# A transformer block with conditioning: the transfers of the weight sums issued by GpSimd at listed steps, and scores of the QKV stage placed mostly among V products

## The chip, the cores and the metric

The kernel runs on one core of a Trainium2 chip. The metric is device time in microseconds (us); lower is better. A core has five engines that run side by side, each with its own in-order queue of instructions: TensorE (PE in the profile; its weight loads are PEld), VectorE (DVE), ScalarE (ACT), GpSimd (POOL) and SyncE (SP). An engine waits at its next instruction until what that one needs is there, and all behind it wait too. That holds for an engine that issues a DMA as well: the transfer itself runs on 16 DMA engines, but its issue stands in the engine's queue. In this kernel SyncE issues nearly all DMAs.

## The reference

One block with adaptive layer norms: D = 512, 16 heads of 32, hidden width 2048, T = 2048 tokens in each of two batches. Cut to what matters:

```python
mod = silu(condition) @ Wada + bada
sh_a, sc_a, gt_a, sh_m, sc_m, gt_m = split(mod, 6)
xm = layernorm(x, g1, be1) * (1 + sc_a) + sh_a
x = x + gt_a * (softmax_causal(q @ k.T * scale) @ v @ Wproj + bproj)   # q, k, v = split(xm @ Wqkv)
xm = layernorm(x, g2, be2) * (1 + sc_m) + sh_m
x = x + gt_m * (gelu(xm @ W1 + b1) @ W2 + b2)
```

All is float32, and the attention is causal within a batch.

## The kernel before

The stages follow one another: QKV of batch 0, attention of batch 0, projection of batch 0, QKV of batch 1, its attention and projection, and then the two MLP layers for all tokens. The change touches the two QKV stages, and through them what is left to the attentions.

**QKV stage (class `Qkv`).** A batch has four groups g of 512 tokens, and a group has 12 steps n; in what follows a step is also counted through the stage, at = 12 g + n, from 0 to 47. Group 0 makes eight columns of Q and K by plain products and then four tiles of V (`values`, L868 on). Groups 1 to 3 make two tiles of V (steps 0 and 1), then two pairs of Q/K columns of four steps each (steps 2 to 5 and 6 to 9), each pair by two sets of seven block products in place of eight (`sevens`, L961 on, so 14 products a pair), and two more tiles of V (steps 10 and 11). The seven products need sums of weights (`weight_sums`, GpSimd, L928, in group 0) and sums of tokens (`token_sums`, GpSimd, L959, made for group g + 1 behind step 10 of group g). VectorE adds the partial products (`total`, L992) and makes the low half of each stored column (`keep`, L855 and L856), which SyncE stores (L861). Behind the first pair, or the first two columns in group 0, SyncE is told to load the keys and queries of this group back in the layout that the scores need (`asked`, `load_keys` L339, `load_queries` L348): the keys wait for the columns' store to land.

**Scores.** The attention needs the maximum of each row of scores ahead of its exponentials. So every score tile is computed once beforehand (`bank`: a product s<-kst,qst on PE into one of two PSUM buffers, and VectorE's maximum, L484, or with the causal mask L479), and a unit's maxima are split into three bf16 parts (`split`, L501 to L505). A unit is four heads and 512 queries; the units of the first four heads have 16, 32, 48 and 64 score tiles (units 0 to 3; unit u needs the keys of groups 0 to u and the queries of group u). The function `among`, called behind each product of the QKV stage, asks the planner (`count`, with a cost of width + 190 per tile, or + 250 with the mask) how many tiles bring the sum of costs up to a goal. Before, it begins at step 2 of each group: group 1 spreads unit 0 evenly over its ten steps, and groups 2 and 3 spread units 1 and 2 evenly over twenty; unit 2 may begin at step 7 of group 2. In attention the planner hands out the rest by due times (`due`): the cost still owed to each later unit over the weight of the steps left.

**Weight sums for the MLP.** The MLP multiplies by sums of quarters of W1 and W2, which are made beside the QKV stages. A quarter (class `Quarters`, 16 in all) is four loads (`load`, L1116, 128 KB each), four sums on GpSimd (`make`, L1128) and one store of 896 KB (`store`, L1136). Class `FirstLayer` then loads a block of W1's quarters (1 MB), makes four sums (L1158) and stores 1.75 MB (w1e, L1190), seven times in batch 1. The rooms in SBUF in which they lie are reused, so that a load waits for the landing of an earlier store. All these transfers are issued by SyncE, in the same queue as the columns' stores, the keys, the queries, the token rows x (L809) and Wada (L1289). The function `also(g, n)`, called at each step, says which of load, make and store runs there: before, by the step's remainder by 4 up to step 29 and by 2 from then on; 13 quarters are done in batch 0 and three, besides the seven W1 blocks, in batch 1. Tiles of batch 1's attention (its exponentials e, written by ScalarE at L619) lie where the two W1 rooms were.

Most instructions of a stage are kept in the order of the program; the loads of keys, queries and x and the columns' stores may be moved by the scheduler, which builds each engine's queue once.

Of the kernel before, what the change touches and what calls it, by code (L numbers as in the profile page):

```python
# [8 lines left out]
F32 = mybir.dt.float32  # L9
# [18 lines left out]
def dit_block_kernel(  # L28
# [768 lines left out]
    class Qkv:  # L797
# [241 lines left out]
        def run(self, hp, also):  # L1039
# [3 lines left out]
            for g in range(NG):  # L1043
# [26 lines left out]
                def among(n, k):  # L1070
                    if g > 0 and n >= 2:


                        past = 4 * (n - 2) + k + 1
                        if g == 1:
                            row.score(row.count(cum[0] * past / 40, 0))
                        else:
                            past += 40 * (g - 2)
                            row.score(
                                row.count(  # L1080
                                    cum[0] + (cum[2] - cum[0]) * past / 80,
                                    1 if g == 2 and n < 7 else 2,
                                )
                            )

# [9 lines left out]
    class Quarters:  # L1095
# [9 lines left out]
        def load(self, room):  # L1105
# [3 lines left out]
            for n, i, k in ((A11, 0, 0), (A12, 0, 1), (A21, 1, 0), (A22, 1, 1)):  # L1109
                if f < FC // 2:  # L1110
                    at = (f + i * FC // 2) * P
                    src = w1_v[:, k * C // 2 : (k + 1) * C // 2, at : at + P]
                else:
                    src = w2_v[:, f - FC // 2 + k * FC // 2, i * D // 2 : (i + 1) * D // 2]
                    src = src.rearrange("p (c d) -> p c d", d=P)
                act(nc.sync.dma_start(w[:, n], src))  # L1116
            self.loaded.append((f, w))
# [13 lines left out]
        def store(self):  # L1131
# [3 lines left out]
            act(  # L1135
                nc.sync.dma_start(  # L1136
                    dst.rearrange("p n c d -> p (n c) d"),
# [29 lines left out]
    class FirstLayer:  # L1167
# [8 lines left out]
        def load(self):  # L1176

            act(load_blocks(nc.sync, self.rooms[self.at % 2], 1, self.at))
            self.at += 1
# [8 lines left out]
        def store(self):  # L1188

            act(nc.sync.dma_start(w1e[self.stored], self.rooms[self.stored % 2]))  # L1190
            self.stored += 1
# [66 lines left out]
    with pool("wada") as wp, pool("qkv0") as qp, pool(  # L1258
# [108 lines left out]

        free, early = 2 * (C * 2 + MTT) + 5, 13

        def also(g, n):  # L1370

            at = g * (C * 2 + MTT) + n
            if 11 <= at <= free:
                if at % 4 == 3:
                    quarters.load(room[0])
                elif at % 4 == 0:
                    quarters.make()
                elif at % 4 == 1 and quarters.made:
                    quarters.store()
            if at >= free:  # L1380
                if at == free:
                    w = wp.tile([P, 2 * C * D], F32, tag="wada", name="w7")
                    room[:] = [w[:, k * piece : (k + 1) * piece] for k in range(2)]
                if at % 2 == 1 and quarters.at < early:
                    quarters.load(room[quarters.at % 2])
                elif at % 2 == 0:
                    if quarters.made:
                        quarters.store()
                    if quarters.loaded:
                        quarters.make()  # L1390
            if g == 0 and n == 2:
# [20 lines left out]
    with pool("qkv1") as qp, pool("ps_qkv1", bufs=6, space=PSUM) as ps_mm:  # L1412
# [20 lines left out]
        with pool("hl1") as hp:  # L1433
# [7 lines left out]
            def also(g, n):  # L1441
                at = g * (C * 2 + MTT) + n
                if at in (0, 1, 6):
                    quarters.load(part[(quarters.at - early) % 2])
                if at in (1, 2, 11):
                    quarters.make()
                if at in (3, 4, 13):
                    quarters.store()
# [6 lines left out]

            late_loads = (11, 15, 22, 26, 35, 39, 43)
            qkv.run(hp, also)
# [689 lines left out]
```

## Time and profile before

| | us |
|---|---|
| median of 3 runs | 2315.2 |
| lowest and highest of them | 2313.03, 2316.77 |
| profiled execution, its own time | 2319.8 |
| profiled execution, span from first to last instruction | 2318.1 |
| QKV stage of batch 0 (18.5 to 222.8 of the span) | 204.3 |
| attention of batch 0 (222.8 to 717.3) | 494.5 |
| QKV stage of batch 1 (805.1 to 995.3) | 190.2 |
| attention of batch 1 (995.3 to 1498.3) | 503.0 |
| rest behind it (1498.3 to 2318.1) | 819.8 |

How the rows are read. A row of the windows view has a stretch, its length, and for PE, PEld, DVE, ACT and POOL the busy us and the number of instructions, then the granted share of the TensorE clock, the DMA engines' busy share and GB/s. A row of the groups view has line, engine, operation, out<-in, shapes and count; then busy us and the mean in ns; then the engine's idle time just before these instructions, and what ended most of it. A row of the timeline has start, length, engine, line, operation and, in brackets, a longer idle time before it with what ended it. A row of the waits view has who waited for whom, the us in total, how many times and the longest. SPq and POOLq are queues that issue DMAs; a float32 matmul is recorded as two halves.

### The profile page before, as it was taken

Reading aid. Unit: us, or ns where it says so; the run is one execution under the profiler, and the core shown is the slowest. Engines: PE = TensorE matmul, PEld = TensorE weight load, DVE = VectorE, ACT = ScalarE, POOL = GpSimd, SP = SyncE. Lnnn points to the kernel's source line nnn. Section 1 sums busy time; section 2 is a strip of 40 time slices with the busy share of each in tenths; the row PEclk is TensorE's granted clock in tenths of the full one; section 3 lists DMA queues with packets and bytes.
Section 4 is the critical chain, followed back from the end, with each engine's and each line's share of the span. In section 5 each row is a group of like instructions: output and inputs, shape, how many; then the busy total and the mean of one; then the engine's idle time right before and its main releaser. Section 6 shows DMA issues by size and latency. Waiting matters only on the chain. (4 is left out here: it accounts for less than half of the span.)

```text
span 2318.1 us, 34368 instructions
## 1 busy us (share of the span) xinstructions
PE 2248.9 (97%) x12429; PEld 1443.0 (62%) x12429; DVE 1560.1 (67%) x3132; ACT 981.8 (42%) x1908; POOL 1279.0 (55%) x998
## 2 busy tenths in 40 slices
PE   8979999999999999999999999999999999999998
PEld 4656545555444456744455545446888888788887
DVE  3467776767765525766677677555896876877787
ACT  3323555555556134245555555632332242252230
POOL 3233787878884453258798787654764602602510
PEclk9999999999999999999999999999999999999999
DMA  7888605151143679781321513265375654554643
GB/s 255 250 229 255 131 24 119 47 118 43 35 141 108 237 224 315 243 228 33 79 68 34 123 29 126 90 216 199 121 273 205 208 176 156 199 174 152 216 144 116
DMA packets 153858, 355.66 MB, mean 153 GB/s; under 512 B 14496, under 2 KB 56012, under 8 KB 138968
## 3 DMA queue, kind: packets, MB, share of 16 engines
q1 hardware_dynamic: 151296, 336.90, 48.3%
q0 software_dynamic: 2016, 16.02, 1.7%
q8 instruction: 98, 1.61, 0.3%
q14 instruction: 72, 0.59, 0.1%
q10 hardware_dynamic: 376, 0.55, 0.1%
HBM read 253.80 MB, written 107.48 MB: 156 GB/s over the span
## 5 line engine op out<-in xcount | busy, mean ns | idle before, releaser
L619 ACT ACTIVATE e<-st 128x512 f32<-128x512 f32 (+1 forms) x1152 | 573.7, 578 | 404.5 <-PE st L204 357.3
L484 DVE TENSOR_REDUCE mx<-s 128x1 f32<-128x512 f32 x612 | 413.3, 687 | 225.3 <-PE s L204 223.8
L649 POOL TENSOR_TENSOR ee<-ee,e 128x1024 f32<-128x1024 f32 x212 | 499.0, 2388 | 7.7 <-ACT e L619 7.7
L204 PE MATMUL s<-kst,qst 128*128 128x512 f32 (+3 forms) x1032 | 438.1, 427 | 30.6 <-DMA qst<-q 11.5
L204 PE MATMUL st<-qst,kst 128*128 128x512 f32 (+3 forms) x1280 | 402.5, 379 | 0.0
L204 PE MATMUL ps_a<-sum,room 128*128 128x256 f32 x1504 | 358.3, 382 | 6.6 <-DVE c L1630 3.8
L204 PEld LDWEIGHTS ps_a<-sum,room 128*128 128x128 f32 x1504 | 282.3, 191 | 56.5 <-issue 8.7
L204 PE MATMUL o<-e,vv 128*32 128x512 f32 (+3 forms) x2560 | 301.8, 539 | 0.9 <-POOL e L628 0.9
L479 DVE CUSTOM_DVE_ANT_0 junk<-s,causal 128x128 bf16<-128x128 f32 (+3 forms) x420 | 205.9, 490 | 121.9 <-PE s L204 114.3
L204 PEld LDWEIGHTS s<-kst,qst 128*128 128x128 f32 x1032 | 195.1, 189 | 138.1 <-issue 45.5
L204 PEld LDWEIGHTS st<-qst,kst 128*128 128x128 f32 x1280 | 230.6, 189 | 68.6 <-issue 39.4
L649 POOL TENSOR_TENSOR ee<-e 128x1024 f32<-128x1024 f32 x84 | 198.2, 2383 | 119.3 <-ACT e L619 119.2
L204 PEld LDWEIGHTS <-sel 32*128 32x128 bf16 x1152 | 29.6, 91 | 196.0 <-issue 192.3
L628 POOL TENSOR_SCALAR_AFFINE_SELECT e<-e 128x256 f32<-128x256 f32 x256 | 104.4, 441 | 84.9 <-ACT e L619 51.9
L1858 POOL TENSOR_TENSOR c<-c,h 128x512 f32<-128x512 f32 x40 | 58.3, 1480 | 160.9 <-ACT c L1856 160.9
L204 PE MATMUL ps_b<-sum,room 128*128 128x256 f32 x608 | 143.6, 379 | 0.0
L204 PE MATMUL st<-fold,sel 32*128 32x512 bf16 (+1 forms) x1152 | 119.1, 373 | 8.6 <-ACT e L619 4.3
L204 PEld LDWEIGHTS ps_b<-sum,room 128*128 128x128 f32 x608 | 115.0, 190 | 15.4
L1128 POOL TENSOR_TENSOR w<-w 128x256 f32<-128x256 f32 x64 | 45.2, 729 | 142.0 <-DMA w<-in_L_cond_W_dram 130.2
L204 PEld LDWEIGHTS o<-e,vv 128*32 128x32 f32 x2560 | 61.4, 108 | 99.3 <-issue 80.3
L204 PE MATMUL ps_v<-wqkv,xmT 128*128 128x512 f32 x256 | 118.2, 597 | 0.0
L484 DVE TENSOR_REDUCE mx<-st 128x1 f32<-128x512 f32 x156 | 107.0, 686 | 3.8 <-PE st L204 1.3
(227 smaller groups left out, 3216.2 us busy)
## 6 DMA issues: line engine op xcount, KB each, us to landing
qst<-q SPq DMA_DIRECT2D x128, 256.0 KB
room<-w1e SPq DMA_DIRECT2D x28, 1024.0 KB
kst<-k SPq DMA_DIRECT2D x24, 1024.0 KB
room<-w1e SPq DMA_DIRECT2D x28, 768.0 KB
room<-w2e SPq DMA_DIRECT2D x21, 1024.0 KB
q<-hl SPq DMA_DIRECT2D x32, 512.0 KB
k<-hl SPq DMA_DIRECT2D x32, 512.0 KB
room<-w2e SPq DMA_DIRECT2D x21, 768.0 KB
```

Source lines behind the costliest of these rows:

```text
L204: return tc.keep_in_program_order(nc.tensor.matmul(*args, **kw))
L479: nc.vector.tensor_tensor_reduce(junk[:, :w], s[:, :w], causal[:, QB - w :], 1.0, MASKED, ALU.add, ALU.max, m,)
L484: nc.vector.tensor_reduce(m, s[:, :w], axis=AX.X, op=ALU.max)
L619: act(nc.scalar.activation(e[:, h % 2, :w], sts[h][:, :w], AF.Exp))
L628: nc.gpsimd.affine_select(d, d, pattern=[[0, 2], [1, P]], compare_op=ALU.is_ge, fill=0.0, base=0, channel_multiplier=-1,)
L649: act(engine.tensor_tensor(dst, x, y, ALU.add))
L1128: act(nc.gpsimd.tensor_tensor(w[:, n], w[:, x], w[:, y], op))
L1858: nc.gpsimd.tensor_tensor(c, c, piece_of(base, i, t, pair), ALU.add)
```

## The change

1. The loads and stores of `Quarters` and `FirstLayer` are issued by GpSimd instead of SyncE.
2. In batch 0 the steps of load, make and store are three lists, with 11 quarters instead of 13; the first is loaded at step 5 instead of 11. Within a step a store comes first, then a sum, then a load.
3. Batch 1 makes five quarters instead of three, and the W1 blocks are loaded at other steps; the last at 39 instead of 43, so its store stands at 43 instead of 47.
4. `among` begins at step 0 of groups 1 to 3. A V step counts three times a Q/K step: a group is 20 parts, of which the four V steps have 3 each and the eight Q/K steps 1 each. Group 1 still scores unit 0; groups 2 and 3 score unit 1 and, by cost, two thirds of unit 2; the rest goes to attention. Unit 2 may begin at step 8 of group 2.

```diff
                 def among(n, k):
-                    if g > 0 and n >= 2:
-                        past = 4 * (n - 2) + k + 1
-                        if g == 1:
-                            row.score(row.count(cum[0] * past / 40, 0))
-                        else:
-                            past += 40 * (g - 2)
-                            row.score(
-                                row.count(
-                                    cum[0] + (cum[2] - cum[0]) * past / 80,
-                                    1 if g == 2 and n < 7 else 2,
-                                )
-                            )
+                    if g == 0:
+                        return
+                    half = MTT // 2
+                    values = min(n, half) + max(0, n - half - 2 * C)
+                    past = 3 * values + min(max(0, n - half), 2 * C)
+                    among_values = n < half or n >= half + 2 * C
+                    past = (past + (3 if among_values else 1) * (k + 1) / 4) / 20
+                    if g == 1:
+                        row.score(row.count(cum[0] * past, 0))
+                        return
+                    goal = cum[1] + (cum[2] - cum[1]) * 2 // 3
+                    row.score(
+                        row.count(
+                            cum[0] + (goal - cum[0]) * (past + g - 2) / 2,
+                            1 if g == 2 and n < 8 else 2,
+                        )
+                    )
...
-                act(nc.sync.dma_start(w[:, n], src))
+                act(nc.gpsimd.dma_start(w[:, n], src))
...
-                nc.sync.dma_start(
+                nc.gpsimd.dma_start(
                     dst.rearrange("p n c d -> p (n c) d"),
...
-            act(load_blocks(nc.sync, self.rooms[self.at % 2], 1, self.at))
+            act(load_blocks(nc.gpsimd, self.rooms[self.at % 2], 1, self.at))
...
-            act(nc.sync.dma_start(w1e[self.stored], self.rooms[self.stored % 2]))
+            act(nc.gpsimd.dma_start(w1e[self.stored], self.rooms[self.stored % 2]))
...
-        free, early = 2 * (C * 2 + MTT) + 5, 13
+        free, early = 2 * (C * 2 + MTT) + 5, 11
+        loads = (5, 11, 15, 19, 23, 27, 29, 30, 35, 36, 40)
+        makes = (7, 12, 16, 20, 24, 28, 31, 32, 37, 38, 42)
+        stores = (9, 13, 17, 21, 25, 29, 33, 33, 39, 40, 44)
...
-            if 11 <= at <= free:
-                if at % 4 == 3:
-                    quarters.load(room[0])
-                elif at % 4 == 0:
-                    quarters.make()
-                elif at % 4 == 1 and quarters.made:
-                    quarters.store()
-            if at >= free:
-                if at == free:
-                    w = wp.tile([P, 2 * C * D], F32, tag="wada", name="w7")
-                    room[:] = [w[:, k * piece : (k + 1) * piece] for k in range(2)]
-                if at % 2 == 1 and quarters.at < early:
-                    quarters.load(room[quarters.at % 2])
-                elif at % 2 == 0:
-                    if quarters.made:
-                        quarters.store()
-                    if quarters.loaded:
-                        quarters.make()
+            if at == free:
+                w = wp.tile([P, 2 * C * D], F32, tag="wada", name="w7")
+                room[:] = [w[:, k * piece : (k + 1) * piece] for k in range(2)]
+            for step, steps in (
+                (quarters.store, stores), (quarters.make, makes),
+                (lambda: quarters.load(room[quarters.at % len(room)]), loads),
+            ):
+                for _ in range(steps.count(at)):
+                    step()
...
-                if at in (0, 1, 6):
+                if at in (0, 1, 6, 7, 14):
                     quarters.load(part[(quarters.at - early) % 2])
-                if at in (1, 2, 11):
+                if at in (1, 2, 11, 12, 16):
                     quarters.make()
-                if at in (3, 4, 13):
+                for _ in range((3, 4, 13, 13, 18).count(at)):
                     quarters.store()
...
-            late_loads = (11, 15, 22, 26, 35, 39, 43)
+            late_loads = (11, 20, 23, 27, 31, 35, 39)
```

A W1 block that is loaded at step a is summed at a + 2 and stored at a + 4, before and after.

## The prediction, on record before the run

> **What bounds the kernel now.** First the page's busy line, then the busy time of each engine by stage (QKV stage of batch 0, its attention, QKV stage of batch 1, its attention).
>
> ```profile
> span 2318.1 us, 34368 instructions
> PE 2248.9 (97%) x12429; PEld 1443.0 (62%) x12429; DVE 1560.1 (67%) x3132; ACT 981.8 (42%) x1908; POOL 1279.0 (55%) x998
> ```
>
> ```profile
> core 0: us, PE busy (x) PEld busy (x) DVE busy (x) ACT busy (x) POOL busy (x), PEclk, DMA share, GB/s
> 18.50:222.80 204.30, 188.36 (x713) 122.78 (x713) 102.49 (x262) 66.24 (x141) 60.69 (x77) 0.97 0.82 240
> 222.80:717.30 494.50, 486.09 (x3436) 247.81 (x3435) 340.24 (x846) 284.59 (x570) 394.70 (x272) 1.00 0.35 88
> 805.10:995.30 190.20, 184.12 (x674) 121.12 (x672) 98.66 (x252) 64.04 (x137) 69.69 (x68) 0.99 0.80 261
> 995.30:1498.30 503.00, 490.27 (x3436) 250.26 (x3435) 340.63 (x848) 285.03 (x570) 392.11 (x268) 0.99 0.34 85
> ```
>
> PE is the bound everywhere: only time in which it stands idle or runs at a lowered clock can be won. The QKV stages leave it idle for 204.3 - 188.4 = 15.9 and 190.2 - 184.1 = 6.1 us; the two attentions do the same work in 494.5 and 503.0 us, so the second loses 8.5. Which waits these are, the groups of instructions in the first QKV stage (two rows), the second and the second attention say:
>
> ```profile
> L204 PE MATMUL s<-kst,qst 128*128 128x512 f32 (+2 forms) x96 | 53.1, 567 | 14.3 <-DMA qst<-q 11.5 <-DVE mx L484 2.2 <-DVE mx L479 0.6
> L204 PE MATMUL ps_mod<-wada,sc 128*32 128x512 f32 x32 | 3.8, 598 | 1.5 <-DVE mx L484 1.5
> ```
>
> ```profile
> L204 PE MATMUL s<-kst,qst 128*128 128x512 f32 (+2 forms) x96 | 53.1, 563 | 5.7 <-DVE mx L484 2.5 <-DVE mx L479 2.1 <-DVE mhl L505 1.1
> ```
>
> ```profile
> L204 PE MATMUL st<-fold,sel 32*128 32x512 bf16 (+1 forms) x540 | 56.6, 374 | 6.3 <-ACT e L619 4.1 <-DVE mhl L505 1.4 <-DMA q<-hl 0.4
> ```
>
> So: one wait of 11.5 for a load of queries, waits for VectorE's maxima of 2.2 + 0.6 + 1.5 = 4.3 and 5.7, and one of 4.1 as the second attention begins. Behind the longer waits the clock is halved; the stretches behind them, by window:
>
> ```profile
> 164.00:167.50 3.50, 3.45 (x6) 2.05 (x7) 1.59 (x4) 0.00 (x0) 2.23 (x4) 0.51 1.12 363
> ```
>
> ```profile
> 918.30:921.80 3.50, 3.50 (x10) 2.76 (x10) 1.69 (x5) 1.07 (x2) 0.94 (x1) 0.51 0.94 376
> ```
>
> 3.5 us at half the clock cost 1.7 in either. The second attention's halved clock is inside its 8.5. The ceiling of the change is 15.9 + 1.7 + 6.1 + 1.7 + 8.5 = 33.9 us.
>
> **The change part by part.**
>
> **(A) The wait for queries, -13.2 before a remainder.** Its PE row, what SyncE issued just before it, and SyncE's waits in this stage:
>
> ```profile
> 164.05 1.19 PE L204 MATMUL s<-kst,qst 128*128 128x512 f32 x2 [11.47 <-DMA qst<-q]
> ```
>
> ```profile
> 134.49 0.37 SPq L861 DMA_DIRECT2D k<-hl  x1
> ...
> 140.48 0.48 SPq L339 DMA_DIRECT2D kst<-k  x1
> 145.25 0.53 SPq L1136 DMA_DIRECT2D w1d<-w  x1
> 145.87 3.85 SPq L1116 DMA_DIRECT2D w<-in_L_cond_W_dram  x4
> 149.76 1.42 SPq L339 DMA_DIRECT2D kst<-k  x3
> 151.22 2.70 SPq L348 DMA_DIRECT2D qst<-q  x4
> ```
>
> ```profile
> SPq L1116 <- DMA w1d<-w: 21.5, 6, 6.5
> ```
>
> Unit 2's keys were ready to load at 140.48, but a store and a load of the W sums stood in between in SyncE's queue, and the other three quarters of the keys left at 149.76. With the W transfers on GpSimd, keys and queries follow one another: 140.48 + 1.9 + 2.7, so the last is issued at about 145 instead of 153.9. It landed at 164.0, 10 us behind its issue; at the same distance it lands at 155. The other half of the change moves the need: by the planner's costs the first score of unit 2 stood in step 10 of group 2 and now stands in the last slot of step 11, behind some 6 V products (0.87 each, below) and 5 scores; less 8 scores and 2.7 of VectorE waits that drop out before it, this is 152.6 + 6.2 - 1.8 - 2.7 = 154.3. So load and need meet: I keep 1 us of the wait, within 0 to 11 (the load lands no earlier than now).
>
> **(B) Waits for VectorE in the QKV stages, -9.3.** A window of group 3 (180 to 213) prices VectorE's part of a score:
>
> ```profile
> L484 DVE TENSOR_REDUCE mx<-s 128x1 f32<-128x512 f32 x20 | 13.6, 686 | 10.5 <-PE s L204 10.4
> L479 DVE CUSTOM_DVE_ANT_0 junk<-s,causal 128x512 bf16<-128x512 f32 (+3 forms) x10 | 4.9, 486 | 1.1 <-PE s L204 0.9
> L992 DVE TENSOR_TENSOR ps_w<-ps_w,x 128x256 f32<-128x256 f32 x8 | 3.4, 431 | 1.3 <-PE ps_w L204 0.9
> L856 DVE SCALAR_TENSOR_TENSOR hl<-ps_w,hl 128x512 fp32r<-128x512 f32 x3 | 2.0, 682 | 0.0
> ```
>
> About 0.65 a score. A pair of Q/K columns (4 steps, 14 products) has six sums of 0.43 and four remainders of 0.68, 5.3 us, and had 16 scores, 10.4: 15.7 us of VectorE beside some 15.5 of PE, (14 x 0.87 and 16 x 0.21, both from the rows under D), with two PSUM buffers for scores. By the new fractions (a V step 3/20, a Q/K step 1/20) a pair has about 7 scores in groups 2 and 3: 4.6 + 5.3 = 9.9 beside 13.6 of PE. A V step has 5 or 6: 3.6 beside 4.6. So these waits go but for the first V step behind the pairs (step 10), where four remainders are still in VectorE's queue when scores come thick: 0.6 in each of four groups, 2.4 kept. 4.3 + 5.7 + 1.7 of clock - 2.4 = 9.3; ends: all 11.7 gone, or, if V steps queue as pairs did, only 5.
>
> **(C) Start of the second attention, -8.2.** The row of ScalarE, and SyncE's:
>
> ```profile
> 1003.12 1.09 ACT L619 ACTIVATE e<-st 128x512 f32<-128x512 f32 x2 [4.78 <-DMA w1e<-w]
> ```
>
> ```profile
> 994.64 0.33 SPq L1190 DMA_DIRECT2D w1e<-w  x1
> ```
>
> The exponentials are written where the last W1 sum still lay, whose store left at 994.64, in step 47. The list of loads now ends at 39, so the last store is in step 43, four steps earlier (two of Q/K and two of V, some 3.5 and 4.6 us each: 16 us), and 8.5 us of transfer fit. I count 8.2 of 8.5; if the chain of loads and stores slips to the end, 0.
>
> **(D) 15 scores of each batch go to attention, 0.** By the planner's costs the QKV stage scores 81 instead of 96; ten of the 15 land in the two first steps of unit 4, which had none. What one costs PE, among V products and in attention, and V products alone:
>
> ```profile
> 170.81 0.79 PE L204 MATMUL s<-kst,qst 128*128 128x512 f32 x1
> 171.89 0.79 PE L204 MATMUL s<-kst,qst 128*128 128x512 f32 x1
> ```
>
> ```profile
> 234.83 0.39 PE L204 MATMUL s<-kst,qst 128*128 128x512 f32 x1
> 235.06 0.40 PE L204 MATMUL st<-qst,kst 128*128 128x512 f32 x1
> 173.55 7.03 PE L204 MATMUL ps_v<-wqkv,xmT 128*128 128x512 f32 x16
> ```
>
> 16 half products of V alone take 7.03, 0.87 a product; with a score the period is 171.89 - 170.81 = 1.08, so 0.21 a score. In attention it is 235.06 - 234.83 = 0.23. 30 x 0.02 is under 1 us. VectorE is busy for 340 of 494 us there and takes 15 x 0.65 = 10 more; were it not hidden, up to +10 an attention, but its row leaves room: 0, within 0 and +5.
>
> **(E) Work wanted earlier, +2.5.** Scores now also stand in steps 0 and 1, 7 us (16 half V products) ahead of their first place. The queries of unit 1, issued behind its keys, and its first score:
>
> ```profile
> 96.83 2.74 SPq L348 DMA_DIRECT2D qst<-q  x4
> ...
> 113.37 0.59 PE L204 MATMUL s<-kst,qst 128*128 128x512 f32 x1
> ```
>
> Wanted at 106.4, issued by 99.6: if they took 10 us as unit 2's, they come at 109.6, 3 late; W transfers no longer ahead of them take some off. I put 1 us each on three such places (A has the fourth's), less what batch 1 has spare: 2.5, within 0 and 8.
>
> **(F) GpSimd's queue, 0.** DMAs that it issues today, the first token sum of group 2, and the product that needs it:
>
> ```profile
> L1555 POOL DMA_DIRECT2D w2e<-room x7 | 4.1, 579 | 2.1 <-POOL room L1158 1.8 <-PE ps_b L204 0.3
> L816 POOL DMA_DIRECT2D wqkv<-in_L_cond_Wqkv_dram x3 | 2.4, 800 | 0.0
> ```
>
> ```profile
> 114.00 1.27 POOL L959 TENSOR_TENSOR vv<-xmT 128x512 f32<-128x512 f32 x1
> ```
>
> ```profile
> 115.33 1.13 PE L204 MATMUL ps_w<-vv,qst 128*128 128x256 f32 x4
> ```
>
> A quarter is four loads and a store, 5 x 0.6 to 0.8 = 3 to 4 us of GpSimd; 16 quarters and seven pairs of W1 transfers come to some 65 us of an engine that is idle for 144 and 121 of the two stages' us. What queues behind: a load waits for the room's store to land, a sum for its load, and behind both stand the token sums (L928's weight sums in group 0). These are issued behind step 10, and the first product that reads one comes three V steps and two products later, 12 us; today the first ends at 115.3 as its product starts. In batch 0 the new lists put no load between step 20's sum and step 22's token sums; in batch 1 a load stands there, behind the store of step 18. So they should come earlier than today. 0, within 0 and +46 (the rival below).
>
> The Trainium skill, SBUF — State Buffer, section SBUF: two separate sides, says that a DMA issued from GpSimd can stand still while VectorE runs a copy in its two-port mode, since its descriptors are not written. No row shows such a hold; by it (F) would grow, and the sum with it.
>
> Sum: -13.2 + 1 - 9.3 - 8.2 + 0 + 2.5 + 0 = -27.2. The profiled execution took 2319.8 (span 2318.1 and 1.7 around it), 4.6 above the median of 2315.2; 2319.8 - 27.2 = 2292.6 there, and **2288.0** against the median.
>
> **The rivals.** *All idle time goes*: -33.9, 2281. *The loads of (A) land no earlier*, since traffic and not the order of issue sets them: DMA share is 0.82 in that stage. The wait would then be 164.0 - 154.3 = 9.7 and the halved clock stays: 11.4 instead of 1, 2298. For it speaks the share, against it the 9 us between 140.48 and 149.76, in which the keys were not even issued. The Trainium skill, DMA: Bandwidth & Descriptors, section Issuing engines are not separate DMA queues, says that DMAs of all issuers run on the same 16 engines and that a second issuer saves only issue time; by that rule it is this rival. *(C) or (E) fails*: the last store is late, or loads are late at all four early places by 3 us: 2296 to 2297. *GpSimd makes it slower*: its queue holds the token sums back behind a landing. Place: the first product with a token sum in groups 1 to 3 of both batches; slack about 10 us; beyond it every us is PE's. Six times 6 us and a halved clock behind each (1.7) are 46: 2334. It decides from a landing some 16 us behind its issue; unit 2's queries took 10. *Nothing comes of it*: waits of equal size elsewhere, 2315.
>
> **How the numbers follow.** Forecast (2283 to 2294) 0.52; all gone 0.08; (A), (C) or (E) partly failing (2294 to 2306) 0.25; nothing 0.07; slower 0.08. The range 2280 to 2302 leaves out the upper part of the third case and the last two, 0.2. A measurement of this kernel tells about 0.2% (4.6 us) from no change: faster 0.87, same 0.05, slower 0.08.
>
> **What would show it.** (A): no idle row of over 2 us before a score around 150 to 165, keys and queries issued back to back. (B): idle time from mx and mhl in the QKV stages falls from 10 to about 2.5 us. (C): the two attentions within 1 us of each other. (D): attention of batch 0 stays at 494 to 496. (E): idle from qst or kst before the first scores of group 2 or 3. (F): idle of ps_w<-vv from a POOL sum; POOL rows of DMA issue well over 0.8 us. Wrong if new idle time in the QKV stages exceeds 10 us.

## The result, and the profile after

The changed kernel takes 2292.4 us (median of 5 runs, 2290.6 to 2294.4) beside 2314.0 for the kernel before, run on the same chip: a ratio of 0.9904, 95% interval 0.989 to 0.9919, or 21.6 us less. The forecast was 2288.0. The profiled execution took 2294.4 (span 2292.7), 25.4 less than that of before.

The page of the changed kernel, its span and busy line:

```profile
span 2292.7 us, 34383 instructions
PE 2239.8 (98%) x12429; PEld 1439.5 (63%) x12429; DVE 1560.2 (68%) x3132; ACT 979.7 (43%) x1908; POOL 1342.7 (59%) x1092
```

PE's busy share rises from 97 to 98%; GpSimd (POOL) has 63.7 us more, which are the issues of W transfers. By stage (QKV stage and attention of batch 0, then of batch 1; columns as in the prediction):

```profile
18.10:208.30 190.20, 185.02 (x698) 121.05 (x698) 95.86 (x241) 66.14 (x141) 98.56 (x128) 0.98 0.83 247
208.30:705.40 497.10, 488.94 (x3451) 249.92 (x3450) 349.11 (x868) 284.18 (x570) 391.88 (x268) 1.00 0.34 86
793.20:979.10 185.90, 179.15 (x659) 118.91 (x658) 91.23 (x231) 64.06 (x138) 98.77 (x115) 0.99 0.89 292
979.10:1475.90 496.80, 488.74 (x3450) 249.93 (x3449) 348.71 (x868) 283.57 (x570) 391.90 (x268) 1.00 0.33 83
```

Against the rows of before, the four stages stand at -14.1, +2.6, -4.3 and -6.2. The rest behind them took 816.8 instead of 819.8, though nothing in it was changed: in the profiled execution of before a wait of 2.36 us stands there, which this one lacks. Of the twelve profiled executions in this document six have such a wait, so it is chance. PE's idle time in the first QKV stage fell from 15.9 to 5.2 us; in the second it rose from 6.1 to 6.75. The groups of the scores (first and second QKV stage, second attention) say which waits went and which came:

```profile
L204 PE MATMUL s<-kst,qst 128*128 128x512 f32 (+2 forms) x81 | 50.1, 636 | 5.1 <-DMA qst<-q 4.9
```

```profile
L204 PE MATMUL s<-kst,qst 128*128 128x512 f32 (+2 forms) x81 | 49.0, 623 | 5.9 <-DMA qst<-q 4.1 <-issue 1.6
```

```profile
L204 PE MATMUL st<-fold,sel 32*128 32x512 bf16 (+1 forms) x540 | 54.0, 372 | 1.4 <-DVE mhl L505 0.6 <-ACT vv L873 0.6
```

VectorE's maxima and remainders, 4.3 and 5.7 us of waiting before, are gone from both stages, and so is ScalarE's 4.1 at the start of the second attention. What is left are loads of queries. In PE's timeline of the changed kernel these are the first scores of unit 1 and of unit 2 in batch 0, then in batch 1:

```profile
110.16 0.87 PE L204 MATMUL s<-kst,qst 128*128 128x512 f32 x2 [3.52 <-DMA qst<-q]
162.70 0.47 PE L204 MATMUL s<-kst,qst 128*128 128x512 f32 x1 [1.41 <-DMA qst<-q]
```

```profile
881.74 0.53 PE L204 MATMUL s<-kst,qst 128*128 128x512 f32 x2 [1.64 <-issue]
931.45 0.76 PE L204 MATMUL s<-kst,qst 128*128 128x512 f32 x1 [4.13 <-DMA qst<-q]
```

Three of the four were not there before; they are new. The clock is halved behind two of them (columns as above, the 0.50 is the granted clock):

```profile
108.60:115.40 6.80, 5.24 (x9) 3.00 (x10) 1.76 (x5) 0.00 (x0) 5.62 (x5) 0.50 1.04 403
931.30:934.70 3.40, 3.25 (x5) 1.83 (x6) 1.01 (x2) 0.00 (x0) 0.00 (x0) 0.50 1.05 425
```

PE's work from 110.16 to 115.4 at half the clock costs 2.6, that from 931.45 to 934.7 costs 1.6. SyncE's queue before unit 2's first score of batch 0:

```profile
141.08 4.95 SPq L339 DMA_DIRECT2D kst<-k  x4
146.07 2.93 SPq L348 DMA_DIRECT2D qst<-q  x4
```

Keys and queries do leave back to back, the last by 149 instead of 153.9. But they landed at 162.7, only 1.4 earlier than before (164.0): 13.7 us behind the last issue instead of 10.1. Beside them GpSimd issued a store and seven loads of a quarter, 1.75 MB:

```profile
139.97 1.08 POOL L1139 DMA_DIRECT2D w1d<-w  x1 [1.06 <-issue]
140.99 4.98 POOL L1119 DMA_DIRECT2D w<-in_L_cond_W_dram  x7
```

### The profile page after: what moved, and what is told of

It reads as the page before. It is cut to its first block, busy times and chain, and to the rows that moved or that the text cites. A ratio compares the mean times of both kernels' runs of the same rounds, so it can differ in the third digit from the quotient of the medians.

```text
span 2292.7 us, 34383 instructions
## 1 busy us (share of the span) xinstructions
PE 2239.8 (98%) x12429; PEld 1439.5 (63%) x12429; DVE 1560.2 (68%) x3132; ACT 979.7 (43%) x1908; POOL 1342.7 (59%) x1092
## 5 line engine op out<-in xcount | busy, mean ns | idle before, releaser
L484 DVE TENSOR_REDUCE mx<-s 128x1 f32<-128x512 f32 x606 | 409.4, 688 | 199.8 <-PE s L204 198.0
L479 DVE CUSTOM_DVE_ANT_0 junk<-s,causal 128x512 bf16<-128x512 f32 (+3 forms) x422 | 207.0, 490 | 116.3 <-PE s L204 108.4
L628 POOL TENSOR_SCALAR_AFFINE_SELECT e<-e 128x256 f32<-128x256 f32 x256 | 103.7, 433 | 119.1 <-ACT e L619 116.8
L204 PE MATMUL ps_v<-wqkv,xmT 128*128 128x512 f32 x256 | 126.3, 606 | 0.0
L1500 POOL TENSOR_TENSOR sum<-xm 128x256 f32<-128x256 f32 x16 | 15.6, 972 | 152.8 <-PE ps_a L204 152.8
```

The lines of the kernel that those rows point to most:

```text
L204: return tc.keep_in_program_order(nc.tensor.matmul(*args, **kw))
L479: nc.vector.tensor_tensor_reduce(junk[:, :w], s[:, :w], causal[:, QB - w :], 1.0, MASKED, ALU.add, ALU.max, m,)
L484: nc.vector.tensor_reduce(m, s[:, :w], axis=AX.X, op=ALU.max)
L628: nc.gpsimd.affine_select(d, d, pattern=[[0, 2], [1, P]], compare_op=ALU.is_ge, fill=0.0, base=0, channel_multiplier=-1,)
L1500: act(engine.tensor_tensor(dst, x, y, ALU.subtract))
```

## The experiments

The theory is that of the prediction: SyncE's queue held the keys and queries back, the placing of scores removes VectorE's waits, an earlier last store frees the second attention. Rival 1: unit 2's wait went because its need moved. Rival 2: traffic sets the landing, whoever issues. Lengths of the stages are read off each trace from the first product of a stage to the first of the next; ratios are to the kernel before, run on the same chip (changes in us are (ratio - 1) x 2315).

| kernel | us | ratio, 95% | QKV 0 | att. 0 | QKV 1 | att. 1 |
|---|---|---|---|---|---|---|
| before | 2314 to 2316 | 1 | 204.3 | 494.5 | 190.2 | 502.9 |
| changed | 2292.4 | 0.9904 (0.989 to 0.9919) | 190.1 | 497.1 | 186.0 | 496.7 |
| queue alone | 2313.8 | 0.9989 (0.998 to 0.9998) | 196.7 | 506.2 | 191.2 | 493.5 |
| scores alone | 2312.5 | 0.9986 (0.9975 to 0.9996) | 195.7 | 498.8 | 182.2 | 507.9 |
| changed, old scores | 2303.0 | 0.9945 (0.9933 to 0.9958) | 194.4 | 494.6 | 195.2 | 493.6 |
| changed, SyncE issues | 2296.7 | 0.9912 (0.9898 to 0.9925) | 189.7 | 497.6 | 180.6 | 502.5 |
| changed, unit 1 later | 2284.9 | 0.9869 (0.9855 to 0.9882) | 183.1 | 497.3 | 180.3 | 496.8 |
| changed, W1 blocks apart | 2300.4 | 0.994 (0.9928 to 0.9953) | 190.4 | 497.3 | 191.1 | 496.7 |
| changed, Wada later | 2313.7 | 0.9998 (0.9986 to 1.0011) | 209.8 | 497.3 | 186.2 | 496.7 |
| changed, all of unit 2 scored | 2308.2 | 0.9974 (0.996 to 0.9989) | 198.0 | 494.7 | 196.2 | 494.2 |
| unit 1 later, SyncE issues | 2297.0 | 0.9916 (0.9902 to 0.9931) | 193.6 | 497.0 | 180.8 | 502.0 |
| unit 1 later, W1 blocks a little apart | 2288.2 | 0.988 (0.9864 to 0.9897) | 185.3 | 497.2 | 181.4 | 496.7 |

Four of these profiled executions (queue alone, old scores, unit 1 later with SyncE issuing, W1 blocks a little apart) have 3.4 us at half the clock from about 19 us on, at most 1.7 us of their QKV 0. No edit touches that place, and the others lack it.

### The queue alone

```diff
 # in the kernel before: the four issues, nothing else
-                act(nc.sync.dma_start(w[:, n], src))
+                act(nc.gpsimd.dma_start(w[:, n], src))
```

> The kernel before, with one part of the change alone: the loads and stores of the W1 and W2 sums are issued by GpSimd instead of SyncE, at the old steps and with the old placing of scores. Theory (the queue of SyncE held unit 2's keys and queries back behind W transfers): the wait of 11.5 us before unit 2's first score falls to 4 us or less and its halved clock shrinks with it, while the waits for VectorE's maxima (4.3 and 5.7) and the 8.5 of the second attention stay: 2303 to 2305. Rival 1 (the wait went only because the need came later): it stays at 11 or grows little less, 2314. Rival 2 (traffic sets the landing, whoever issues): it stays at 9 to 11, 2312 to 2315.

The wait did what the theory said, the total (2313.8, theory 2303 to 2305) did not. SyncE's queue and PE in that kernel:

```profile
140.54 1.75 SPq L339 DMA_DIRECT2D kst<-k  x4
142.34 3.17 SPq L348 DMA_DIRECT2D qst<-q  x3
```

```profile
155.91 1.19 PE L204 MATMUL s<-kst,qst 128*128 128x512 f32 x2 [2.79 <-DMA qst<-q]
...
233.68 2.27 PE L204 MATMUL o<-e,vv 128*32 128x512 f32 x8 [9.66 <-POOL e L628]
```

With the need unmoved (153.1; before 152.6), keys and queries issued some 8 us sooner landed 8 us sooner: 11.47 became 2.79, and rival 2 falls for this place. The second attention lost nothing any more (493.5), though the last store still stood in step 47. But the first attention got 11.7 us longer. GpSimd's rows there:

```profile
228.94 2.88 POOL L1128 TENSOR_TENSOR w<-w 128x256 f32<-128x256 f32 x4 [0.89 <-DMA w<-in_L_cond_W_dram]
232.12 1.07 POOL L1136 DMA_DIRECT2D w2d<-w  x1 [0.30 <-POOL w L1128]
233.13 2.96 POOL L628 TENSOR_SCALAR_AFFINE_SELECT e<-e 128x256 f32<-128x256 f32 x8
```

GpSimd also masks the attention's exponentials (L628), and these stood in its queue behind the thirteenth quarter: its sums, which wait for its loads, and its store. PE waited 9.66 us, and the clock was halved for 10.2 from 227.0 on. The prediction's rival for GpSimd has this mechanism at another place (it named the token sums).

### The scores alone

```diff
 # in the kernel before: among() of the changed kernel, nothing else
-                    if g > 0 and n >= 2:
+                    if g == 0:
+                        return
...
```

> The kernel before, with the new placing of scores alone (81 of 96 in the QKV stage, most of them in V steps); the W transfers stay on SyncE at the old steps. Theory: the waits for VectorE's maxima in both QKV stages go (-11.7); the wait before unit 2's first score stays at 9 to 10 (its need is only 1 to 2 us later); the second attention still loses 8.5; early waits for keys or queries cost 3 to 6: 2305 to 2309. Rival 1 (the later need was what took the wait away): unit 2's wait is under 3 here too, 2296 to 2300. Rival 3 (scores in V steps only move VectorE's waits to other places): waits for the maxima stay above 6, 2312 or more.

Unit 2's wait is gone here too, as rival 1 had it, but rival 1's time (2296 to 2300) is not reached. The wait has in part only moved to unit 1: the first score of unit 2 stands at 161.1, where in before PE was ready for it at 152.6, and of these 8.5 us the new early wait (3.97) and the halved clock behind it (about 2.4) are 6.4. The placing itself moved the need by some 2 us, as the theory said. The early wait, and another:

```profile
110.30 0.87 PE L204 MATMUL s<-kst,qst 128*128 128x512 f32 x2 [3.97 <-DMA qst<-q]
204.53 0.79 PE L204 MATMUL s<-kst,qst 128*128 128x512 f32 x1 [4.13 <-DVE mx L479]
```

The second, the only wait for a maximum, is not VectorE's load, as the name suggests, so rival 3 falls though the total (2312.5) is in its range. ScalarE's row (it makes the high half of a column) shows what VectorE stood behind, a column's store that had not landed so that its buffer was not free:

```profile
200.05 0.60 ACT L855 ACTIVATE hl<-ps_w 128x512 fp32r<-128x512 f32 x1 [3.20 <-DMA k<-hl]
```

In SyncE's queue W transfers stood ahead of these stores: the low halves of this pair's columns were done by 185.8, and this column's store was issued at 194.3. So the queue delays stores too, not only keys. The second attention takes 507.9: ScalarE waits there for a W1 store that left at 985.9, behind the start of the attention (982.4).

```profile
994.31 1.08 ACT L619 ACTIVATE e<-st 128x512 f32<-128x512 f32 x2 [9.15 <-DMA w1e<-w]
```

### The changed kernel with the old scores, and with SyncE issuing

> The changed kernel with the old placing of scores: GpSimd issues the W transfers at the new steps, but 96 scores are spread evenly again from step 2 on. Theory: unit 2's wait is at 0 to 4, the second attention's 8.5 is gone with the last store at step 43, the waits for the maxima (10 and its halved clock) are back, and unit 1's early wait of 3.5 is not there since its first score stands where it stood before: 2294 to 2298. Rival 1: unit 2's wait is back at 9 or more: 2304 to 2306. Should the early waits come from GpSimd's transfers being in flight and not from the earlier need, they stay here too: 2299 or more.

> The changed kernel with all W transfers issued by SyncE again, at the new steps and with the new placing of scores. Theory: the waits for the maxima and the second attention's loss stay won (-20), but keys and queries stand behind W transfers in SyncE's queue: unit 2's wait is 6 to 10 and unit 1's 3.5 to 7, each with a halved clock: 2300 to 2306. Rival 1 or rival 2 (who issues makes no difference): 2291 to 2294, with waits as in the changed kernel.

Old scores: no early wait of unit 1, unit 2's in batch 0 at 1.82, the attentions at 494.6 and 493.6, so the new steps cured what the queue alone had broken at the start of the first attention. But the QKV stage of batch 1 takes 5.0 more than before, and its group of scores shows why the total missed the theory:

```profile
L204 PE MATMUL s<-kst,qst 128*128 128x512 f32 (+2 forms) x96 | 53.3, 566 | 9.9 <-DMA qst<-q 5.1 <-DVE mx L479 3.3 <-DVE mx L484 1.5
```

A wait of 5.1 for unit 2's queries with the old placing: in batch 1 this wait does not come from an earlier need. So unit 1 speaks against the expectation's last sentence (its wait went with the earlier need), and unit 2 of batch 1 for it.

SyncE issuing: at 2296.7 it lies between the theory and its rivals. The QKV stage of batch 0 is as short as in the changed kernel (no wait for unit 2, 5.41 for unit 1), and that of batch 1 is 5.4 shorter, with 1.57 for unit 2. What is lost is the second attention: ScalarE's exponentials wait for the last W1 sum again, and the clock is halved for 10 us from 979.8 on, 502.5 in all:

```profile
978.74 1.09 ACT L619 ACTIVATE e<-st 128x512 f32<-128x512 f32 x2 [1.88 <-DMA w1e<-w]
```

So the new steps without the queue win only a part of term (C): beside the scores alone (502.5 against 507.9, both with SyncE and the new placing), 5.4 us. The last W1 store left SyncE 7.8 us ahead of the attention here and 3.5 us behind its start there. The queue without the steps wins all of it (493.5): GpSimd, in whose queue that store has no columns, keys and queries ahead of it, sent it 21.8 us ahead of the attention, though it is the same step 47 as before. The theory's reason for (C) is neither the only one nor the larger.

Read across, these four kernels price the new lists of steps, which no run has alone. By the ratios they are worth 10.2 us with GpSimd issuing and the old scores (old scores against queue alone), and 17.1 with SyncE issuing and the new ones (SyncE issuing against scores alone). The new scores are worth 9.5 (changed against old scores). The move to GpSimd, between the changed kernel and that with SyncE issuing, comes to 1.9 by the ratios: it wins 5.8 in the second attention and loses 5.4 in the QKV stage ahead of it, and the intervals overlap, so that with the new steps and scores it can't be told from nothing.

### Unit 1 later

```diff
-                    past = (past + (3 if among_values else 1) * (k + 1) / 4) / 20
+                    past = past + (3 if among_values else 1) * (k + 1) / 4
+                    past = (past if g == 1 else max(0, past + 20 * (g - 2) - 4.5)) / (20 if g == 1 else 35.5)
...
-                            cum[0] + (goal - cum[0]) * (past + g - 2) / 2,
+                            cum[0] + (goal - cum[0]) * past,
```

> The changed kernel, but the scores of unit 1 begin in group 2 only with the second half of step 1 (the same 65 scores spread over 35.5 parts in place of 40, so that unit 2 too begins some three slots later). Theory (the loads land when traffic lets them, and only the need moved ahead of it): the wait of 3.5 us with its halved clock (2.7) in batch 0 goes, so do the 1.4 there and the 1.6 in batch 1, and of the 4.1 with 1.6 of halved clock in batch 1 some three quarters: 12 to 13 us off, 2279 to 2282. Rival 1: the denser scores bring VectorE's waits back, 2284 to 2289. Rival 2: the loads are held by what they queue behind and land later by as much, 2290 to 2293.

The QKV stages (rows of this kernel):

```profile
17.80:200.80 183.00, 182.01 (x698) 119.70 (x698) 94.11 (x240) 66.00 (x142) 95.40 (x125) 1.00 0.85 258
785.90:966.20 180.30, 177.12 (x659) 118.15 (x658) 90.29 (x230) 63.56 (x138) 98.80 (x115) 1.00 0.91 302
```

They are 7.0 and 5.7 shorter than in the changed kernel, 12.7 in all, as the theory had it. What idle time is left is 1.0 a stage for VectorE's maxima and 1.9 before unit 2 in batch 1, with the clock at 1.00 throughout. The median is 7.5 lower (8.1 by the ratios), less than these stages say, since a wait of 2.4 as in the rest of before stood in this profiled execution and not in that of the changed kernel, and single executions differ by some 2 us. With 2284.9 it misses the theory's 2279 to 2282 and lies in the range of rival 1, whose waits are 1.0 a stage. Nor did the need alone move: without the stop at unit 1 the loads of unit 2 in batch 0 were issued by 139.9 instead of 149.0, ahead of the W transfers that left beside them in the changed kernel, and landed before PE wanted them. It is the fastest of all versions here; its interval lies wholly below that of the changed kernel.

### W1 blocks apart

```diff
-            late_loads = (11, 20, 23, 27, 31, 35, 39)
+            late_loads = (11, 19, 20, 30, 32, 36, 39)
```

> The changed kernel, but in batch 1 the W1 blocks are loaded at steps 11, 19, 20, 30, 32, 36, 39 instead of 11, 20, 23, 27, 31, 35, 39, so that no block's store and load (2.75 MB) leave just ahead of unit 2's keys. Theory (that traffic makes the keys and queries land 16 us behind their issue there): they land 8 to 10 us behind it, the wait of 4.1 and its halved clock (1.6) go, and the QKV stage of batch 1 takes 180 to 181 instead of 186: 2286 to 2288. Rival 1: the landing has nothing to do with the W1 blocks, 2291 to 2293. Rival 2: the sums, now bunched in steps 19 to 24, hold GpSimd's token sums back: a wait of a product for a token sum, 2294 or more.

In the changed kernel, GpSimd issued 2.75 MB just ahead of unit 2's keys of batch 1, which SyncE issued from 911.51 on:

```profile
909.63 0.57 POOL L1166 DMA_DIRECT2D w<-w1d  x1
910.19 0.54 POOL L1193 DMA_DIRECT2D w1e<-w  x1
```

The first score that needed them stood at 931.45, 20 us after the first key's issue. With the blocks apart there is no wait before unit 2's first score. That alone shows little, since a longer wait at unit 1 brings PE there 4.2 us later (931.5 instead of 927.3). The landing shows the theory's claim: by the semaphore updates in the traces the last query landed 15.6 us behind its issue in the changed kernel and 9.2 here, as in the kernel before (9.1). The transfers in flight made them late. At 2300.4 the kernel is slower than the theory and rival 1 gave, and rival 2's range holds it, but no product waits for a token sum. The stage is 5 us longer, since the blocks had to go somewhere: 3.98 before unit 1's first score (1.64 before), and 5.57 near the end, where ScalarE again waits for a column's store while W1 blocks are in flight:

```profile
974.84 0.60 ACT L855 ACTIVATE hl<-ps_u 128x512 fp32r<-128x512 f32 x1 [5.10 <-DMA k<-hl]
```

With the blocks only a little apart, on top of the later unit 1, it went the same way:

```diff
-            late_loads = (11, 20, 23, 27, 31, 35, 39)
+            late_loads = (11, 20, 22, 30, 31, 35, 39)
```

> The kernel of the run with later scores, but in batch 1 the third and fourth W1 blocks are loaded at steps 22 and 30 instead of 23 and 27, so that only one store, and no load, leaves just ahead of unit 2's keys. Theory (what is in flight ahead of the keys delays them by some 6 us): the wait of 1.9 us before unit 2's first score in batch 1 goes and nothing else moves: 2282 to 2284. Rival 1: two sums of 5 us now stand ahead of the token sums of step 34, or the blocks crowd behind step 30 and the columns' stores land late, and a new wait of 2 to 6 us appears: 2285 to 2290.

Unit 2's wait of 1.9 is gone and one of 2.04 for VectorE stands at 961.0 instead: rival 1. The stage takes 181.4 against 180.3; whether this version is slower at all than the one with unit 1 later can't be told, as their intervals overlap.

### Wada later

```diff
                     ins = nc.sync.dma_start(w[:, n, k, :], wada_v[:, k, s * D : (s + 1) * D])
+                    if s0 == 3:
+                        act(ins)
...
+            elif g == 1 and n == 10:
+                load_wada(3, 4)
...
-                if g == 1:
-                    load_wada(3, 4)
```

> The changed kernel, but the last 2 MB of Wada, which SyncE issues ahead of unit 1's keys and queries, are issued behind them (step 22 of batch 0 instead of step 16, and kept there). Theory (traffic already in flight sets when unit 1's queries land, 110 us into the span in every run so far though they were issued between 97 and 103): they land at 104 to 107, the wait of 3.5 and its halved clock (2.7) fall to 0 to 1: 2286 to 2288. Rival 1: the W quarter in flight and not Wada holds them, 2291 to 2293. Rival 2: Wada now comes late to its own products some 20 us later, a new wait there, 2293 or more.

PE in this kernel, and GpSimd:

```profile
108.77 0.54 PE L204 MATMUL s<-kst,qst 128*128 128x512 f32 x2 [1.68 <-DMA qst<-q]
141.16 2.07 PE L204 MATMUL ps_w<-vv,qst 128*128 128x256 f32 x4 [22.05 <-POOL vv L959]
```

```profile
132.89 2.81 POOL L1119 DMA_DIRECT2D w<-in_L_cond_W_dram  x4 [4.67 <-DMA w1d<-w]
137.81 2.07 POOL L1131 TENSOR_TENSOR w<-w 128x256 f32<-128x256 f32 x3 [2.10 <-DMA w<-in_L_cond_W_dram]
139.85 1.25 POOL L959 TENSOR_TENSOR vv<-xmT 128x512 f32<-128x512 f32 x1
```

Unit 1's queries came only 1.4 us earlier (108.77 against 110.16) with 2 MB less ahead of them, so Wada is not the main thing that holds them; which transfers are was not shown. The edit also made the scheduler put the token sums behind two more W quarters in GpSimd's queue: the first began at 139.85, where in the changed kernel it is at 109.16. PE waited 22 us and the stage grew by 19.7. This is the prediction's rival for GpSimd at the very place that it named; the total says nothing on Wada.

### All of unit 2 scored

```diff
-                    goal = cum[1] + (cum[2] - cum[1]) * 2 // 3
+                    goal = cum[2]
```

> The changed kernel, but all of unit 2 is scored in the QKV stage again (96 scores instead of 81, still three times as dense in V steps). Tests what the 15 scores that went to attention are worth. Theory (a score costs PE the same in either place, and what counts is VectorE's cover in the stage): each attention is 2.5 to 3 us shorter and each QKV stage 3 longer by PE, and waits for the maxima of 1 to 4 us a stage come back: 2293 to 2299. Rival (scores are dearer in attention, and V steps still cover them): 2288 to 2291.

Its rows by stage, and its scores in the first:

```profile
19.30:217.30 198.00, 189.59 (x713) 123.36 (x713) 103.08 (x260) 65.86 (x141) 98.43 (x128) 0.98 0.83 248
217.30:712.00 494.70, 486.06 (x3436) 247.83 (x3435) 340.81 (x848) 284.75 (x570) 391.87 (x268) 1.00 0.33 81
```

```profile
L204 PE MATMUL s<-kst,qst 128*128 128x512 f32 (+2 forms) x96 | 53.7, 586 | 8.4 <-DMA qst<-q 7.2 <-DVE mx L484 0.9
```

Each attention is 2.4 to 2.5 shorter, the QKV stages 7.9 and 10.2 longer. VectorE's waits return only in small part (0.9 here, 1.8 in batch 1, of 10.0 before): the weight on V steps, more than the smaller number, had removed them. But scores that follow one another closer bring unit 2's need forward, onto its load: 4.51 before it instead of 1.41. It is slower than both the theory and its rival gave, since neither had that.

### Unit 1 later, and SyncE issuing

The two edits together: the later scores above, with the four issues back on SyncE.

> The kernel of the run with later scores, but all W transfers issued by SyncE again. It asks what the move to GpSimd is worth once no score is wanted early. Theory (the later need alone takes the waits for keys and queries away, and what only the move wins is the start of the second attention, where the last W1 store stands behind the last keys and queries in SyncE's queue): QKV stages within 2 us of those with later scores (183.1 and 180.3), the second attention 502 to 503 instead of 497: 2289 to 2292. Rival 1 (SyncE's queue still delays keys and queries by more than the slack): waits of 2 us or more before the first scores of unit 1 or unit 2 in batch 0, 2293 to 2298. Rival 2 (the move is worth nothing at all by now): 2284 to 2286.

SyncE's first key for unit 1 in this kernel, behind a store of W sums, and in the one with unit 1 later alone:

```profile
96.86 0.53 SPq L1140 DMA_DIRECT2D w1d<-w  x1
98.69 4.24 SPq L339 DMA_DIRECT2D kst<-k  x4
```

```profile
91.41 2.93 SPq L339 DMA_DIRECT2D kst<-k  x4
```

That store waited 2.2 us for GpSimd's sums, and a load ahead of it 1.9 for a landing. PE in this kernel:

```profile
115.19 0.53 PE L204 MATMUL s<-kst,qst 128*128 128x512 f32 x2 [2.16 <-DMA qst<-q]
120.84 1.99 PE L204 MATMUL ps_w<-vv,qst 128*128 128x256 f32 x8 [1.83 <-POOL vv L959]
166.01 0.77 PE L204 MATMUL s<-kst,qst 128*128 128x512 f32 x1 [2.73 <-DMA qst<-q]
```

Rival 1: SyncE's queue makes the keys 7 us later, unit 1 and unit 2 wait again, and the second attention is 5.2 longer. By the medians the move to GpSimd is worth 12.1 us here (10.9 by the ratios); in the kernel before it was worth 1.6 (2.5), and between the changed kernel and that with SyncE issuing 4.3 (1.9, within the noise). One and the same edit: what it is worth depends on what else would wait.

## Why the prediction was right, and which terms were not

The direction, most of the places and the range were right; by the medians the change won 21.6 us of the 27.2 forecast. Several terms were wrong, and that their errors partly cancelled is luck: (E) came out 11.0 worse, (B) and (D) together 6.1 better, and the rest, which was not changed, gave 3.0 in the profiled executions. The new idle time in the QKV stages (3.52, 1.64 and 4.13, 9.3 in all) stayed just under the 10 that the prediction had named as a sign of being wrong. In the profile:

| term | forecast | measured | from |
|---|---|---|---|
| (A) | -12.2 | -11.8 | 11.47 to 1.41, halved clock (1.7) gone |
| (B) | -9.3 | -11.3 | 10.0 of idle to 0.4, and 1.7 of clock |
| (C) | -8.2 | -8.7 | att. 1 -6.2, less the 2.5 that (D) adds |
| (D) | 0 | -4.1 | QKV -4.3 and -4.9, attentions +2.6 and +2.5 |
| (E) | +2.5 | +13.5 | 3.52 + 2.6, 1.64, 4.13 + 1.6 |
| (F) | 0 | 0 | no wait for GpSimd |
| sum | -27.2 | -22.4 | with -3.0 of the rest: -25.4 |

- **The step that failed: (E), "I put 1 us each on three such places", "within 0 and 8".** It measured 13.5, past its upper bound. Two things stood against it. First, the prediction itself had the need of unit 1 at 106.4 and the landing 3 us behind it, and then took something off for W transfers "no longer ahead of them". They are out of SyncE's queue but still in the DMA engines: the queries landed at 110, as before (109.6 there, by the semaphore updates), and PE waited 3.52. The halved clock, which the prediction counted for (A), was left out for (E); it is 4.2 of the 13.5. Secondly, in batch 1 the changed steps put 2.75 MB of W1 into the engines 1.3 us ahead of unit 2's keys (before, the store left 8 us ahead of them); with the blocks apart the last query landed 9.2 instead of 15.6 us behind its issue, and the old placing of scores kept the wait (5.1). With unit 1 later, the two QKV stages together came down by 12.7.
- **(A) was right in size and half right in cause.** The queue alone removes most of it (2.79 left). The new placing alone leaves nothing, but it mostly moved the wait to unit 1. Together they leave 1.41, since the load gained only 1.4 us here, not 9, with the W transfers beside it; the need was at 161.3 and not at 154.3, and of those 7 us the new wait at unit 1 and its clock are 6.1. The prediction treated the places as independent; a wait at one moves the need at the next. Its rival (A lands no earlier) holds for the landing but not for the time.
- **(B)**: its bound "all 11.7 gone" was the truth within 0.4. The 2.4 kept for step 10 did not appear; the run with all of unit 2 scored (2.7 of such waits) shows that the weight on V steps does most of it.
- **(C)** was right in size, half right in cause. Old steps and GpSimd give 493.5; SyncE and the new placing give 507.9 with the old steps and 502.5 with the new ones. So SyncE's queue alone is enough to explain the loss, and the step alone wins some 5 us of it.
- **(D)**: its 0.02 a score from two rows was too small, and its sign (attention of batch 0 stays at 494 to 496) failed at 497.1. PE's busy time in the QKV stages, less the halved clock, falls from 186.7 to 182.4 and from 182.4 to 177.5: 0.29 and 0.33 a score, where the attentions pay 0.17.
- **(F)** held in the changed kernel: issues of 0.54 to 1.16 us, no product waiting for a token sum. It hangs on the lists of steps, however. With the old steps GpSimd's queue cost 9.66 us and a halved clock at the start of attention, and with the token sums moved behind two quarters 22 us. The prediction's price of 46 was for six such places; one of 22 us was enough to undo the change. The Trainium skill, SBUF — State Buffer, section SBUF: two separate sides, says that a VectorE operation in a two-port mode keeps GpSimd from writing its DMAs' descriptors. None of the 94 issues that were moved took longer than 1.16 us in the changed kernel, so no run here shows such a hold.

The Trainium skill, DMA: Bandwidth & Descriptors, section Issuing engines are not separate DMA queues, has it that DMAs run on the same 16 DMA engines whichever engine starts them, and that starting them from several engines saves only the time of the issue. The runs bear out the first half (2.75 MB issued by GpSimd made SyncE's keys late) and not the second: the move was worth 12.1 us where the keys were otherwise issued 7 us later, because an issue that waits holds back all that stands behind it.

## What to carry to other kernels

Price the parts of a change together, run each alone and leave each out: here the queue alone won 2.5 us and the scores alone 3.2 by the ratios, the whole 22.2, since each part alone made new waits that another part removed. And see whether a wait that is gone from one place stands at another. When transfers are moved to another engine's queue, list what else that engine must do behind a load that has not landed (here masks and token sums), and remember that the bytes are still in the same DMA engines, ahead of whatever is issued next. And when work is moved earlier for the sake of one engine, first check when its data lands: the best version here moved the scores back by one and a half steps and kept all the rest.

## What the runs showed of the hardware beyond that

The same transfers need fewer packets on GpSimd's queue. The DMA part of the page, queue of SyncE (q1) and of GpSimd (q0), before and after:

```profile
q1 hardware_dynamic: 151296, 336.90, 48.3%
q0 software_dynamic: 2016, 16.02, 1.7%
```

```profile
q1 hardware_dynamic: 107040, 293.64, 43.0%
q0 software_dynamic: 10944, 59.28, 7.3%
```

43.26 MB moved over; they were 44256 packets (0.98 KB each) on the one and 8928 (4.8 KB) on the other, at about the same share of time (5.3% less, 5.6% more).

A short wait can halve the clock, and its length does not tell for how long. One of 2.73 us (unit 1 later, SyncE issuing) and one of 2.04 (W1 blocks a little apart) were followed by 3.4 us at half the clock, that of 3.52 by 6.8, and the 1.58 at the start of the second attention (SyncE issuing) by 10.2, while 2.16, 1.93 and 1.68 elsewhere cost none. The Trainium skill, TensorE: Matmul & The Clock Gate, section What's actually happening, gives free-running windows of 3.4 us and one idle window as the condition. The lengths agree (3.4, 6.8, 10.2); the waits of 2.73, 2.04 and 1.58 show that less than a whole idle window was enough.
